# Mixing attention tokens with the images turned through DRAM, squares summed on ScalarE, and weighted products shared between VectorE and GpSimd

## The chip, the cores and the metric

The kernel runs on one core of one Trainium2 chip. The metric is the time of one execution on the device, in microseconds. The profile is one execution on that core, taken by the hardware profiler. Engines are named as the profile names them: PE is TensorE (PEld its weight loads), DVE VectorE, ACT ScalarE, POOL GpSimd, SP the queue from which nearly all DMAs are issued.

## What is computed

The reference is two layers of a "metaformer" on x of shape (4, 32, 128, 128), that is 4 batches of 32 token images of 128 x 128, all in float32. The part that matters here is the attention of the first layer. Cut down, it is

```python
tokens = x.reshape(b * t, 1, H, W)                 # x: normalised along the last axis before
tokens_norm = instance_norm(tokens, norm1_g, norm1_b)
k = fno_layer(tokens_norm, key_w, ...)             # spectral convolution + 1x1 skip, 16 heads
q = fno_layer(tokens_norm, query_w, ...)
v = fno_layer(tokens_norm, value_w, ...)
dprod = softmax(einsum('bhtd,bhsd->bhts', qf, kf) / scale)
attn = einsum('bhts,bhsd->bhtd', dprod, vf)        # tokens of a batch mixed with each other
attn = fno_layer(attn, proj_w, ...)
attn = instance_norm(attn + tokens, attn_norm_g, attn_norm_b)
m = instance_norm(attn, norm2_g, norm2_b)          # then two mixer layers, a recurrent layer,
...                                                # and the second layer of the network
```

The skip paths of value and projection make one linear map between the 32 token images of a batch: every pixel of the new image of token t is a weighted sum over the same pixel of the images s. Together with the residual this is one 128 x 128 matrix, block diagonal with a 32 x 32 block for each batch. The spectral paths add a few low Fourier coefficients to each image; they are kept as coefficients and never as images. The norms that follow need the sum of squares of each mixed image.

## The kernel before

**Layout.** XA is one SBUF tile `[128, 4, 32, 128]`: image row h on the partitions, then batch, token and column w. It holds x, then the normalised x, then the mixed images, all in place. WXY is a second large tile that holds coefficients and weights of this part: Drep (product of value and projection weights, in four head groups g, real and imaginary), Frep (the images' low coefficients, one block for each batch b), PTs (the softmax's weights), and CTbd, the block-diagonal matrix.

**Up to 134 us.** The images are loaded on SP, and in eight half batches of 16 images (`stats`, `normalise`, `transform`, lines 808 to 873) row statistics are taken, each image is normalised in place by ScalarE (L833) or VectorE (L835), and transformed by TensorE (L850). Weights are prepared beside that; their copies md, dd and m1d go by DRAM on SP. `scores` of each batch, the Gram matrix (L936), the softmax (L1004 to L1013) and PTs follow, and last CT is copied into CTbd (L1035).

**Sums stage, 134 to 205 us.** Two jobs run side by side (lines 1275 to 1304). In eight steps (g, x_) VectorE makes four products df, one for each batch, of Drep with Frep (L1290, 128 x 1088 elements, both inputs in SBUF), and TensorE sums them over heads with PTs into four accumulators ps_y (L1303, four column groups at a time). Between the products of a step, two or three times, the generator `mix` is advanced by one chunk of four image columns w:

- TensorE turns four slices `XA[:, :, :, w]` to have images on the partitions (L1050, four transposes), ScalarE copies them out as uT (L1052);
- TensorE multiplies each of the four with CTbd, the slice stationary (L1055), which turns the result back;
- ScalarE copies the 512 columns of pm into XA at stride (L1057), squares pm (L1062), and VectorE adds the square to a running sum (L1063).

`mixed_coefficients` (L1076, L1078), before step (2, 0), applies CTbd to the coefficients. Twenty chunks belong to this stage. The order on each engine is that of the program where `keep_in_program_order` says so, else the scheduler's.

**Norms stage, 205 to 244 us.** `norms` (lines 1082 to 1266) runs the list NORMS, one name after the other; inside `in_order` each compute engine keeps the order of the list (SP is not held by it). T, U, M, C, S, E with a number are a chunk's transposes, copy uT, products, copy back, square and addition for the last 12 chunks; three copies back go to VectorE (BY_VECTOR), and three chunks' squares are summed by TensorE (BY_TENSOR, L1210). The other names are the norm's own work: TY (transpose of YT, L1164), FU (L1121), VA, P0, P1, VB, D0, D1 (products and sums of coefficients on VectorE), NY (L1167) and K on GpSimd, GS and VS (sums on ScalarE, L1132 and L1155), TG (L1146), CH (the variance of every image, L1226 to L1229), PW (a power on GpSimd, L1232), E1, BC, H0, N0. EQ sums the squares over partitions with TensorE.

**After 244 us.** The list MIXERS drives the two mixer layers in eight chunks of four tokens. The first readers of mixed images are Z (L1415, which reads `XA[:, b, tokens, :]`), then TA (L1576) and R (L1583, which also reads xin, the original x, loaded again on SP from L1349). The recurrent layers and the second layer follow.

PSUM and SBUF come from pools; a pool's tile waits until what lay at its place is no longer used.

Of the kernel before, what the change touches and what calls it, by code (L numbers as in the profile page):

```python
# [32 lines left out]
P = 128  # L33
# [92 lines left out]
NORMS = """  # L126
    T31 T20 U31 M31 T27 U20 S31 C31 T24 M20 TY U24 M24 E31 U27 T23 FU C20 VA P0 S24 T28 U23 M27 S20 T26 E20 NY C24
    E24 U28 M23 M28 C23 T25 S23 U26 T29 S27 M26 E23 C27 E27 P1 U25 M25 U29 C26 T21 T30 S26 VB C28 D0 M29 K S28 E28
    U21 M21 C25 S25 U30 E26 S29 T22 D1 E25 C21 M30 WT S21 U22 GS G0 E29 M22 E21 HM W0 EQ VC TG S22 S30 VS W1 C29 E30
    C30 C22 E22 CH PW WV E1 BC H0 KG GI N0 KN  # L130
"""

BY_TENSOR, BY_VECTOR = (22, 27, 30), (21, 23, 28)
# [143 lines left out]
def _network(  # L277
# [268 lines left out]
    PTs = WXY[:, 11072:12096].rearrange("p (a b c) -> p a b c", b=4, c=P)  # L546
    gram = aw.tile([P, NT], F32, name="gram")
# [15 lines left out]
    def big(name):  # L563
        return psb.tile([P, 512], F32, tag="big", name=name)
# [233 lines left out]
    with (  # L798
# [38 lines left out]
        def transform(k):  # L837
# [34 lines left out]
            nc.scalar.copy(dst, p)  # L872
            yield True
# [92 lines left out]

        p = big("ps_s4")[:, :NB]
# [73 lines left out]
    squares = late.tile([P, 4, P], F32, name="squares")  # L1041
    mp = mixing.enter_context(tc.tile_pool(name="mix", bufs=2))
    psm = mixing.enter_context(tc.tile_pool(name="psm", bufs=2, space=PSUM))

    def mix():

        for k, w0 in enumerate(range(0, 80, 4)):
            pt = psm.tile([P, 4, P], F32, tag="pt", name="pt")
            for i in range(4):
                nc.tensor.transpose(pt[:, i, :], XA[:, :, :, w0 + i].rearrange("p b t -> p (b t)"), ident)  # L1050
            uT = mp.tile([P, 4, P], F32, name="uT")
            nc.scalar.copy(uT, pt)  # L1052
            pm = psm.tile([P, 4, P], F32, name="pm")
            for i in range(4):
                mm(pm[:, i, :], uT[:, i, :], CTbd, start=True, stop=True)  # L1055
            dst = XA[:, :, :, w0 : w0 + 4].rearrange("p b t w -> p w (b t)")
            nc.scalar.copy(dst, pm)  # L1057
            if k == 0:
                nc.scalar.square(squares, pm)
            else:  # L1060
                sq = mp.tile([P, 4, P], F32, name="sq")
                nc.scalar.square(sq, pm)  # L1062
                tt(squares, squares, sq, ALU.add)  # L1063
            yield True

    mixed = mix()
# [3 lines left out]
    def mixed_coefficients():  # L1070
        for q in halves(8, 3):
            n = q.stop - q.start
            p = psm.tile([P, 512], F32, tag="pt", name="ps_cf")[:, : 8 * n * KW].rearrange("p (a w) -> p a w", w=KW)
            for b in range(NB):
                c = slice(32 * b, 32 * b + 32)
                mm(p[c], CTbd[c, c], Frep[c, b, q].rearrange("p k r j w -> p (k r j) w"), start=True, stop=True)  # L1076
            for r in range(2):
                nc.scalar.copy(FmT.rearrange("p (r j k) w -> p r k j w", r=2, k=8)[:, r, q],  # L1078
                               p.rearrange("p (k r j) w -> p r k j w", r=2, j=4)[:, r])
        nc.vector.memset(FmT[:, 16, 0:1], 0.0)  # L1080

    def norms(np_, psn):
# [99 lines left out]
        def T(k):  # L1182
            pts[k] = psm.tile([P, 4, P], F32, tag="pt", name="pt")
            for i in range(4):
                nc.tensor.transpose(pts[k][:, i, :], XA[:, :, :, 4 * k + i].rearrange("p b t -> p (b t)"), ident)

        def U(k):
            uTs[k] = mp.tile([P, 4, P], F32, name="uT")
            nc.scalar.copy(uTs[k], pts.pop(k))

        def M(k):
            pms[k] = (psn if k % 3 == 2 else psm).tile([P, 4, P], F32, tag="pm", name="pm")
            u = uTs.pop(k)
            for i in range(4):
                mm(pms[k][:, i, :], u[:, i, :], CTbd, start=True, stop=True)

        def C(k):
            dst = XA[:, :, :, 4 * k : 4 * k + 4].rearrange("p b t w -> p w (b t)")
            if k in BY_VECTOR:
                nc.vector.tensor_copy(dst, pms[k])  # L1200
            else:
                nc.scalar.copy(dst, pms[k])

        def S(k):
            sqs[k] = mp.tile([P, 4, P], F32, name="sq")
            nc.scalar.square(sqs[k], pms[k])

        def sums(q):
            for w in range(4):
                mm(e2[:, 0:1], q[:, w], mean_mat[:, 0:1], start=(summed[0] == 0), stop=(summed[0] == summed[1] - 1))  # L1210
                summed[0] += 1

        def E(k):
            if k in BY_TENSOR:
                sums(sqs.pop(k))
            else:
                tt(squares, squares, sqs.pop(k), ALU.add)

        def EQ():
            sums(squares)  # L1220

        def CH():
            stt(var, e2[:, 0:1], 1.0 / P, var, ALU.mult, ALU.add)  # L1226
# [22 lines left out]
        def N0():  # L1249
# [4 lines left out]
                "WV": WV, "GI": GI, "T": T, "U": U, "M": M, "C": C, "S": S, "E": E, "EQ": EQ, "CH": CH, "PW": PW,  # L1254
# [22 lines left out]
    with (  # L1277
        tc.tile_pool(name="df", bufs=6) as dfp,
# [3 lines left out]
        for g in range(4):  # L1282
            for x_ in range(2):

                df = []
                if (g, x_) == (2, 0):
                    mixed_coefficients()
                for b in range(NB):
                    t = dfp.tile([P, 2, KH * KW], F32, name="df")
                    tt(t.rearrange("p r (k m) -> p r k m", k=8),  # L1290
                       Drep[:, g, :, x_].rearrange("p k j w -> p k (j w)").unsqueeze(1).broadcast_to([P, 2, 8, 4 * KW]),
                       Frep[:, b].rearrange("p k r j w -> p r k (j w)"), ALU.mult)
                    df.append(t.rearrange("p r (k m) -> p r k m", k=8))

                    if b < 2 + (x_ == 0):
                        next(mixed)
                for k in range(4):
                    r, half = divmod(k, 2)
                    m = slice(2 * KW * half, 2 * KW * (half + 1))

                    for b in range(NB):
                        c = slice(32 * b, 32 * b + 32)
                        i = mm(ys[k][c], PTs[:, 1 if (x_ == 1 and r == 0) else 0, g, c],  # L1303
                               df[b][:, r ^ x_, :, m], start=(g == 0 and x_ == 0), stop=(g == 3 and x_ == 1))
                        if k + b > 0:
                            tc.keep_in_program_order(i)
# [1107 lines left out]
```

## Time and profile before

| | us |
|---|---|
| median of 3 runs | 907.72 (907.22 to 908.0) |
| the profiled execution | 908.87 |
| its span in the profile | 907.1 |

| stretch of the span, us | PE | DVE | ACT | POOL | PE clock | GB/s |
|---|---|---|---|---|---|---|
| 100 to 120 | 19.4 | 7.7 | 7.7 | 0.0 | 1.00, 0.83 | 2 |
| 120 to 140 | 13.2 | 14.4 | 8.2 | 0.9 | 0.99, 0.50 | 1 |
| 140 to 200 | 59.2 | 45.0 | 38.4 | 0.0 | 1.00 | 1 |
| 200 to 220 | 16.1 | 16.3 | 12.3 | 7.8 | 1.00, 0.75 | 1 |
| 220 to 240 | 15.1 | 13.2 | 13.7 | 1.2 | 0.73, 0.61 | 1 |

The first table has the times; the profiled execution's own time is 1.77 us over its span, which lies around the recorded instructions. The second has busy microseconds of each engine in each stretch, the TensorE clock that was granted in its halves (1.00 is full), and what the DMA engines moved. A TensorE that shows busy is not at its peak: its instructions overlap, and four products in a row take less than four times the duration of one.

In groups of instructions below, a line gives the source line, engine, operation, output<-inputs, shapes and count; then busy us and mean ns of one; then the engine's idle time before them and what ended it. A line of a timeline gives start, duration, engine, source line, operation, and in brackets the idle time before it and its releaser. The table of stages as printed has the stretch, its length, busy us and count for PE, PEld, DVE, ACT and POOL, the granted clock, the DMA engines' busy share and GB/s.

### The profile page before, as it was taken

The numbers are of one execution on the slowest core, as the hardware profiler recorded it, in microseconds if no ns is written. First come the engines' busy times: TensorE is split into PE (matmuls) and PEld (weight loads), VectorE is DVE, ScalarE is ACT, GpSimd is POOL, SyncE is SP. The second block draws the span as 40 slices with busy tenths as digits, with TensorE's granted clock in tenths as the row PEclk, the third lists the DMA queues.
The fourth block names the chain that finished last, engine by engine and source line by source line (L and its number), as shares of the span: only waits on it lengthen the run. The fifth ranks groups of instructions, "written<-read, shape, count | busy, mean of one in ns | idle before, by whom it ended". The sixth has DMA issues, their size and how long they took to land.

```text
span 907.1 us, 31233 instructions
## 1 busy us (share of the span) xinstructions
PE 807.2 (89%) x12678; PEld 608.8 (67%) x12678; DVE 734.7 (81%) x2352; ACT 666.8 (74%) x1644; POOL 365.2 (40%) x605
## 2 busy tenths in 40 slices
PE   2999969998796989999787988999999999998994
PEld 2656557567663555564435987887878887775994
DVE  5997477777757889989988988987778887777996
ACT  2774636576682779998877997787777877776994
POOL 2000000003143454435521003788896886972263
PEclk9999979997768999999999997999999999999997
DMA  9906000000101101112100000111101111117554
GB/s 228 242 4 125 1 1 1 1 1 1 48 1 48 45 27 48 41 33 70 46 2 1 1 1 4 38 28 39 51 5 50 37 41 39 28 48 248 190 185 143
DMA packets 69419, 49.67 MB, mean 55 GB/s; under 512 B 4561, under 2 KB 64465, under 8 KB 69201
## 3 DMA queue, kind: packets, MB, share of 16 engines
q1 hardware_dynamic: 68929, 47.31, 18.5%
q8 instruction: 102, 1.67, 0.8%
q0 software_dynamic: 288, 0.01, 0.2%
q14 instruction: 52, 0.43, 0.2%
q10 hardware_dynamic: 48, 0.26, 0.1%
HBM read 30.68 MB, written 16.88 MB: 52 GB/s over the span
## 4 chain that ended last, share of the span: by engine, by line
PE 42%; DVE 23%; ACT 11%; POOL 7%; issue 4%; SPq 0%; DVEq 0%; ACTq 0%; POOLq 0%
PE ps_scan L1912 5%; PE ps_k L2065 5%; PE ps_d L2195 4%; DVE XA L1584 4%; DVE XA L1583 4%; ACT WXY L1914 3%; PE ps_y L1303 3%; PE ps_r L2065 2%; PE pm L1055 2%; POOL XN L2044 2%; PE ps_inv L481 2%; PE ps_e L2202 2%; PE ps_st L1426 2%; PE ps_w L2141 2%; ACT yw L1914 2%
## 5 line engine op out<-in xcount | busy, mean ns | idle before, releaser
L2185 DVE SCALAR_TENSOR_TENSOR U<-raw 128x512 f32<-128x512 f32 x128 | 89.6, 728 | 27.9 <-ACT raw L2177 27.6
L1913 DVE SCALAR_TENSOR_TENSOR ps_scan<-WXY,bs,ps_scan 128x128 f32<-128x128 f32 x376 | 105.7, 351 | 1.9 <-PE ps_scan L1912 1.1
L2065 PE MATMUL ps_k<-WXY,q 64*64 64x134 f32 x2048 | 86.4, 282 | 0.9 <-ACT WXY L2149 0.3
L2177 ACT COPY raw<-ps_k 128x512 f32<-128x512 f32 x128 | 71.1, 599 | 17.7 <-PE ps_k L2065 15.0
L2195 PEld LDWEIGHTS ps_d<-WXY,U 128*64 128x64 f32 x2048 | 67.3, 137 | 19.3 <-issue 12.9
L2044 POOL TENSOR_SCALAR xn<-XA,f_r,f_o 128x128 f32<-128x128 f32 x120 | 68.3, 578 | 18.7 <-PE ps_x L2065 14.0
L2044 POOL TENSOR_SCALAR XN<-XA,c_r,c_o 128x128 f32<-128x128 f32 x120 | 73.6, 622 | 5.0 <-issue 2.3
L2195 PE MATMUL ps_d<-WXY,U 128*64 128x67 f32 x2048 | 74.1, 224 | 1.0 <-ACT q L2208 0.5
L2065 PEld LDWEIGHTS ps_k<-WXY,q 64*64 64x64 f32 x2048 | 61.0, 135 | 6.7 <-DVE U L2185 0.8
L2065 PE MATMUL ps_r<-WXY,XN 64*64 64x134 f32 x1024 | 58.4, 289 | 2.4 <-DVE XN L2044 1.3
L850 PE MATMUL ps_st<-cst,XA 128*128 128x130 f32 x256 | 43.7, 311 | 14.3 <-ACT XA L833 11.2
L1641 ACT ACTIVATE xn<-XA,f_o,f_r 128x128 f32<-128x128 f32 x120 | 50.9, 489 | 4.7 <-DVE f_o L1623 4.7
L850 PEld LDWEIGHTS ps_st<-cst,XA 128*128 128x128 f32 x256 | 35.4, 207 | 27.4 <-ACT XA L833 12.3
L1420 ACT ACTIVATE Z<-Z,k,aB 128x128 f32<-128x128 f32 x128 | 51.1, 481 | 3.5 <-DVE Z L1415 3.2
L1583 DVE SCALAR_TENSOR_TENSOR XA<-ps_inv,r1B,xin 128x128 f32<-128x128 f32 x128 | 44.1, 345 | 8.9 <-PE ps_inv L1576 8.9
L1584 DVE SCALAR_TENSOR_TENSOR XA<-Z,gB,XA 128x128 f32<-128x128 f32 x128 | 46.5, 364 | 5.0
L2163 ACT COPY q<-ps_r 128x512 f32<-128x512 f32 x64 | 38.4, 599 | 12.6 <-PE ps_r L2065 12.3
L2024 POOL TENSOR_TENSOR c_r<-c_e,neg_half 128x16 f32<-128x16 f32 (+2 forms) x10 | 25.6, 2564 | 53.6 <-DVE c_e L2017 53.5
L496 PE MATMUL ps_inv<-invq,cst 64*128 64x512 f32 x128 | 41.9, 685 | 4.6 <-ACT invq L487 3.9
L1290 DVE TENSOR_TENSOR df<-WXY 128x1088 f32<-128x1088 f32 x32 | 40.2, 1288 | 2.1 <-PE ps_y L1303 2.1
L2202 PE MATMUL ps_e<-WXY,q 128*64 128x67 f32 x1024 | 41.1, 222 | 0.0
L446 PE MATMUL ps_wx<-xt,wvt 128*128 128x512 f32 x64 | 35.6, 639 | 5.8 <-ACT WXY L453 4.5
(459 smaller groups left out, 2253.7 us busy)
## 6 DMA issues: line engine op xcount, KB each, us to landing
XA<-in_x_dram SPq DMA_DIRECT2D x16, 512.0 KB, 7.1
xin<-in_x_dram SPq DMA_DIRECT2D x32, 256.0 KB, 3.4
turned<-XA SPq DMA_DIRECT2D x32, 256.0 KB, 2.3
out_dram<-res SPq DMA_DIRECT2D x52, 128.0 KB, 2.1
XA<-turned SPq DMA_DIRECT2D x6, 1024.0 KB, 12.2
WXY<-dd SPq DMA_DIRECT2D x4, 544.0 KB, 11.2
XA<-turned SPq DMA_DIRECT2D x6, 256.0 KB, 12.3
out_dram<-resl SPq DMA_DIRECT2D x12, 128.0 KB, 2.1
```

The costliest lines, as they stand in the source:

```text
L850: mm(p[:, i, :], XA[:, b, t0 + j + i, :], cst[:, C_E : C_E + 130], start=True, stop=True)
L1420: nc.scalar.activation(z, z, AF.Gelu, bias=k1, scale=aB[:, j : j + 1])
L1583: stt(a, p2[c, b][:, i], r1B[:, j : j + 1], xin[c, b - b % 2][:, b % 2, i], ALU.mult, ALU.add)
L1584: stt(a, Z[c][:, b, i], gB[c][:, n : n + 1], a, ALU.mult, ALU.add)
L1641: nc.scalar.activation(t[:, dst, :], a, AF.Identity, bias=sh, scale=sc_)
L1913: stt(p4, WX[:, :, h, :], s[:, 0:1], p4, ALU.mult, ALU.add)
L2044: e.tensor_scalar(dst, src_, r, o, ALU.mult, ALU.add)
L2065: m = mm(dst, data, taps, start=(n == 0 and (i, j) not in last), stop=(n == 1), skip_group_check=True)
L2177: nc.scalar.copy(raw[u, k], banks["k", u][:, k])
L2185: stt(U[u][:, k].rearrange("p k s m -> p (k s m)"), v, SLOPE, v, ALU.mult, ALU.max)
L2195: mm(p[HALVES[s], m, b, REACH[k]], U[v][:, b, k, s, HALVES[m]], DR[:, k, REACH[k]], start=(m == 0 and b == 0 and k == 0), stop=(k == 1), s ...
L2202: mm(p[HALVES[j], b * P : b * P + P][:, REACH[m]], q3[v - 1][:, m, b, HALVES[j]], DC[:, m, REACH[m]], start=(b == 0 and m == 0), stop=(m = ...
```

## The change

It rewrites how the images are mixed and who makes the products df. In the text the steps are named by the letters of the new lists.

- **Turning.** Each half batch, once normalised, is also stored to a DRAM tile `normed` (n, h, w). After the last, eight loads of 1 MB bring it back into XA with the images on the partitions: the view XR is `[128 images, 128 rows h, 128 w]`. A chunk k is now four image rows: M is one product, CTbd stationary and 512 columns of XR moving. C copies it back in place; after every 16 rows a 1 MB store takes them to a second DRAM tile, `mixed`. XB, 32 loads of 256 KB, brings all images back with rows h on the partitions, after the last store.
- **Squares.** S squares pm on ScalarE with `accum_out`, one column of `squares` for each chunk; images are on the partitions, so EQ is one reduce of 32 numbers on VectorE.
- **Products.** F n.b is product df of step n and batch b. All of step 0 and batch 3 of every step go to GpSimd, 11 of 32, the others to VectorE. Eight buffers instead of six. Y n.k is one accumulator's part of the sums of step n.
- **Order.** A list SUMS sets the order of the sums stage on every compute engine, and NORMS is written anew. CF is `mixed_coefficients`. XB stands behind S31.

```diff
+SUMS = """
+    F0.3 F0.0 F0.1 F0.2 M0 M1 M2 F1.3 F1.0 F1.1 F1.2 Y0.0 Y0.1 C0 S0 M3 Y0.2 Y0.3 C1 S1 M4 F2.3 F2.0 F2.1 F2.2 Y1.0
+    C2 S2 M5 Y1.1 Y1.2 C3 S3 M6 Y1.3 C4 S4 M7 F3.3 F3.0 F3.1 F3.2 Y2.0 Y2.1 C5 S5 M8 Y2.2 Y2.3 C6 S6 M9 F4.3 F4.0
+    F4.1 F4.2 Y3.0 C7 S7 M10 Y3.1 Y3.2 C8 S8 M11 Y3.3 C9 S9 M12 F5.3 F5.0 F5.1 F5.2 Y4.0 Y4.1 C10 S10 M13 Y4.2 Y4.3
+    C11 S11 M14 CF F6.3 F6.0 F6.1 F6.2 Y5.0 C12 S12 M15 Y5.1 Y5.2 C13 S13 M16 Y5.3 C14 S14 M17 F7.3 F7.0 F7.1 F7.2
+    Y6.0 Y6.1 C15 S15 M18 Y6.2 Y6.3 C16 S16 M19 Y7.0 C17 S17 M20 Y7.1 Y7.2 C18 S18 M21 Y7.3 C19 S19
+"""
 NORMS = """
...
+    TY C20 S20 M22 FU C21 S21 M23 VA C22 S22 M24 P0 NY C23 S23 M25 P1 C24 S24 M26 VB C25 S25 M27 D0 C26 S26 M28 K D1
+    C27 S27 M29 WT C28 S28 M30 GS C29 S29 M31 G0 C30 S30 HM W0 C31 S31 XB EQ VC TG VS W1 CH PW WV E1 BC H0 KG GI N0
+    KN
 """
-BY_TENSOR, BY_VECTOR = (22, 27, 30), (21, 23, 28)
+ROWS = 16
...
+    normed, mixed = (scratch.tile([P, P, P], F32, name=k) for k in ("normed", "mixed"))
+    XR = XA.rearrange("p b t w -> p (b t) w")
...
+            n0 = b * NT + t0
+            nc.sync.dma_start(normed[n0 : n0 + HB].rearrange("n h w -> h n w"), XA[:, b, t0 : t0 + HB, :])
             yield True
...
+        for h in range(0, P, ROWS):
+            nc.sync.dma_start(XR[:, h : h + ROWS, :], normed[:, h : h + ROWS, :])
...
-    def mix():
...
+    psm = mixing.enter_context(tc.tile_pool(name="psm", bufs=4, space=PSUM))
+    squares = late.tile([P, NT], F32, name="squares")
+    junk = late.tile([P, 512], F32, name="junk")
+    pms = {}
+
+    def mix(k):
+        pms[k] = psm.tile([P, 512], F32, tag="pm", name="pm")
+        mm(pms[k], CTbd, XR[:, 4 * k : 4 * k + 4, :].rearrange("p h w -> p (h w)"), start=True, stop=True)
+
+    def mix_copy(k):
+        nc.scalar.copy(XR[:, 4 * k : 4 * k + 4, :].rearrange("p h w -> p (h w)"), pms[k])
+        if (4 * k + 4) % ROWS == 0:
+            h = slice(4 * k + 4 - ROWS, 4 * k + 4)
+            nc.sync.dma_start(mixed[:, h, :], XR[:, h, :])
+
+    def mix_square(k):
+        nc.scalar.activation(junk, pms.pop(k), AF.Square, accum_out=squares[:, k : k + 1])
...
+    def images_back():
+        for t in range(0, NT, TM):
+            for b in range(NB):
+                n = b * NT + t
+                nc.sync.dma_start(XA[:, b, t : t + TM, :], mixed[n : n + TM].rearrange("n h w -> h n w"))
...
-        def T(k):
...
         def EQ():
-            sums(squares)
+            nc.vector.tensor_reduce(total, squares, AX.X, ALU.add)

         def CH():
-            stt(var, e2[:, 0:1], 1.0 / P, var, ALU.mult, ALU.add)
+            stt(var, total, 1.0 / P**2, var, ALU.mult, ALU.add)
...
-        tc.tile_pool(name="df", bufs=6) as dfp,
+        tc.tile_pool(name="df", bufs=8) as dfp,
...
+        def weighted(n, b):
+            g, x_ = steps[n]
+            t = dfp.tile([P, 2, KH * KW], F32, name="df")
+            (nc.gpsimd if n == 0 or b == NB - 1 else nc.vector).tensor_tensor(
+                t.rearrange("p r (k m) -> p r k m", k=8),
+                Drep[:, g, :, x_].rearrange("p k j w -> p k (j w)").unsqueeze(1).broadcast_to([P, 2, 8, 4 * KW]),
+                Frep[:, b].rearrange("p k r j w -> p r k (j w)"), ALU.mult)
+            df[n, b] = t.rearrange("p r (k m) -> p r k m", k=8)
+
+        def summed(n, k):
+            g, x_ = steps[n]
+            r, half = divmod(k, 2)
+            m = slice(2 * KW * half, 2 * KW * (half + 1))
+            for b in range(NB):
+                c = slice(32 * b, 32 * b + 32)
+                mm(ys[k][c], PTs[:, 1 if (x_ == 1 and r == 0) else 0, g, c],
+                   df[n, b][:, r ^ x_, :, m], start=(n == 0), stop=(n == len(steps) - 1))
+
+        with in_order():
+            for piece in SUMS.split():
...
```

More of the change, by code (lines that the diff above doesn't have):

```diff
@@ L119 @@
 """
+SUMS = """
[5 more added lines that the diff above has]
+"""
 NORMS = """
[L127 to L130, printed above, removed]
+    TY C20 S20 M22 FU C21 S21 M23 VA C22 S22 M24 P0 NY C23 S23 M25 P1 C24 S24 M26 VB C25 S25 M27 D0 C26 S26 M28 K D1
+    C27 S27 M29 WT C28 S28 M30 GS C29 S29 M31 G0 C30 S30 HM W0 C31 S31 XB EQ VC TG VS W1 CH PW WV E1 BC H0 KG GI N0
+    KN
 """
-BY_TENSOR, BY_VECTOR = (22, 27, 30), (21, 23, 28)
+ROWS = 16
 MIXERS = """
@@ L546, in _network @@
     PTs = WXY[:, 11072:12096].rearrange("p (a b c) -> p a b c", b=4, c=P)
+    scratch = att.enter_context(tc.tile_pool(name="scratch", bufs=1, space=bass.MemoryType.DRAM))
+    normed, mixed = (scratch.tile([P, P, P], F32, name=k) for k in ("normed", "mixed"))
+    XR = XA.rearrange("p b t w -> p (b t) w")
     gram = aw.tile([P, NT], F32, name="gram")
@@ L1040, in _network @@
     late = mixing.enter_context(tc.tile_pool(name="late", bufs=1))
-    squares = late.tile([P, 4, P], F32, name="squares")
-    mp = mixing.enter_context(tc.tile_pool(name="mix", bufs=2))
-    psm = mixing.enter_context(tc.tile_pool(name="psm", bufs=2, space=PSUM))
-    def mix():
[L1047 to L1066, printed above, removed]
+    psm = mixing.enter_context(tc.tile_pool(name="psm", bufs=4, space=PSUM))
[12 more added lines that the diff above has]
+        nc.scalar.activation(junk, pms.pop(k), AF.Square, accum_out=squares[:, k : k + 1])
     FmT = late.tile([P, 2 * KH, KW], F32, name="FmT")
@@ L1072, in mixed_coefficients @@
             n = q.stop - q.start
-            p = psm.tile([P, 512], F32, tag="pt", name="ps_cf")[:, : 8 * n * KW].rearrange("p (a w) -> p a w", w=KW)
+            p = psm.tile([P, 512], F32, tag="pm", name="ps_cf")[:, : 8 * n * KW].rearrange("p (a w) -> p a w", w=KW)
             for b in range(NB):
@@ L1095, in norms @@
         pool, pools = nc.gpsimd.tensor_tensor, nc.gpsimd.tensor_scalar
-        pts, uTs, pms, sqs = {}, {}, {}, {}
         e2 = psn.tile([P, 512], F32, name="ps_e2")
-        summed = [0, 4 + 4 * len(BY_TENSOR)]
+        total = np_.tile([P, 1], F32, name="total")
         def weighted(o, total, t):
@@ L1179, in GI @@
             ts(gI, ident, scalar("attn_norm_g"), None, ALU.mult)
-        def T(k):
[L1183 to L1217, printed above, removed]
         def EQ():
-            sums(squares)
+            nc.vector.tensor_reduce(total, squares, AX.X, ALU.add)
         def CH():
-            stt(var, e2[:, 0:1], 1.0 / P, var, ALU.mult, ALU.add)
+            stt(var, total, 1.0 / P**2, var, ALU.mult, ALU.add)
             ts(vs[:, 1:2], var, g2e, 1e-10, ALU.mult, ALU.add)
@@ L1253, in norms @@
                 "HM": HM, "TG": TG, "VA": VA, "VB": VB, "VS": VS, "VC": VC, "W1": W1, "TY": TY, "NY": NY, "WT": WT,
-                "WV": WV, "GI": GI, "T": T, "U": U, "M": M, "C": C, "S": S, "E": E, "EQ": EQ, "CH": CH, "PW": PW,
+                "WV": WV, "GI": GI, "M": mix, "C": mix_copy, "S": mix_square, "EQ": EQ, "XB": images_back, "CH": CH, "PW": PW,
                 "E1": E1, "BC": BC, "H0": H0, "N0": N0}
@@ L1281, in _network @@
         ys = [psy.tile([P, 8, 2 * KW], F32, name=f"ps_y{k}") for k in range(4)]
[L1282 to L1286, printed above, removed]
-                    mixed_coefficients()
[L1288 to L1306, printed above, removed]
@@ new lines, in _network @@
+        df, steps = {}, [(g, x_) for g in range(4) for x_ in range(2)]
+        def weighted(n, b):
[6 more added lines that the diff above has]
+            df[n, b] = t.rearrange("p r (k m) -> p r k m", k=8)
@@ new lines, in summed @@
+        def summed(n, k):
[8 more added lines that the diff above has]
+            for piece in SUMS.split():
+                if piece == "CF":
+                    mixed_coefficients()
+                    continue
+                name = piece.rstrip("0123456789.")
+                {"F": weighted, "Y": summed, "M": mix, "C": mix_copy, "S": mix_square}[name](
+                    *map(int, piece[len(name) :].split(".")))
```

## The prediction

> **What bounds the kernel now.** I read the table of stages first (busy time per engine over stretches of the span), then for the two stages that the diff touches the chain of work, the groups of instructions and the timeline. The touched part runs from 133.2 us, when the weights of attention are final, to 244.4 us, when the first mixer reads a mixed image. Everything later (663 us) is untouched. The chain over the start of that part, and the costliest groups from 133.5 to 205 us:
>
> ```profile
> by line: PE pm L1055 41.0%; PE ps_y L1303 27.8%; PE pt L1050 22.1%; ACT sq L1062 2.6%; DVE WXY L1018 2.3%; ACT XA L1057 2.3%; ACT uT L1052 1.7%; issue 1.4%
> ```
>
> ```profile
> L1290 DVE TENSOR_TENSOR df<-WXY 128x1088 f32<-128x1088 f32 x32 | 40.2, 1288 | 2.1 <-PE ps_y L1303 2.1
> L1303 PE MATMUL ps_y<-df,WXY 128*32 128x272 f32 x256 | 27.8, 397 | 0.0
> L1057 ACT COPY XA<-pm 128x512 f32<-128x512 f32 x20 | 21.2, 1059 | 17.7 <-PE pm L1055 17.7
> L1063 DVE TENSOR_TENSOR squares<-squares,sq 128x512 f32<-128x512 f32 x19 | 13.1, 690 | 13.0 <-ACT sq L1062 12.9
> L1062 ACT ACTIVATE sq<-pm 128x512 f32<-128x512 f32 x19 | 12.3, 645 | 0.0
> ```
>
> Three engines share this stage: VectorE has 53 us of work in 70 (df and squares), ScalarE about 51, and TensorE runs transposes, products and sums in one queue; each waits for another in turn (ACT 17.7 us for pm, DVE 12.9 us for sq). No engine is full, and the ring of waits costs 8.9 us a step (eight steps in 71 us). The second stage, 205.2 to 244.4 us, ends like this:
>
> ```profile
> 205.21 2.31 DVE L1164 STREAM_TRANSPOSE WXY<-YT 128x2048 f32<-128x2048 f32 x1 [0.53 <-ACT YT L1314]
> ...
> 231.78 2.31 DVE L1146 STREAM_TRANSPOSE WXY<-HT 128x2048 f32<-128x2048 f32 x1
> ...
> 232.25 2.81 ACT L1202 COPY XA<-pm 128x512 f32<-128x512 f32 x3
> ...
> 244.37 0.75 DVE L1415 SCALAR_TENSOR_TENSOR Z<-XA,sc,ps_inv 128x512 f32<-128x512 f32 x1 [0.77 <-PE ps_inv L496]
> ```
>
> From the end of the second transpose (234.1) to Z a chain of small steps takes 10.3 us; the change leaves it alone. What comes before is the remaining 11 to 12 chunks of the mixing, threaded through VectorE's norm work: the last three copies back stand at 232.25 beside the second transpose, so both lists end together there.
>
> The change puts the same kind of product on GpSimd and on VectorE at once, so I looked for a place where both now read SBUF together:
>
> ```profile
> 207.62 3.13 POOL L1167 TENSOR_SCALAR WXY<-WXY 128x1024 f32<-128x1024 f32 x1 [2.00 <-DVE WXY L1164]
> 208.02 2.15 DVE L1121 TENSOR_TENSOR FuT<-FmT,YT 128x1088 f32<-128x1088 f32 x1
> ...
> 210.40 1.29 DVE L1149 TENSOR_TENSOR V<-FmT,FuT 128x1088 f32<-128x1088 f32 x1
> ```
>
> The same VectorE shape takes 2.15 us beside a GpSimd instruction and 1.29 alone: 0.86 lost to the neighbour.
>
> **What the Trainium skill says.** "SBUF — State Buffer", section "Who interferes with whom": a VectorE instruction with two SBUF inputs contends with a GpSimd instruction that reads SBUF, and the pair of ports is an exclusive lock, not a division of bandwidth. The lines above agree (2.15 against 1.29); so does the line L2044 on GpSimd, 0.44 us at the median and up to 1.73. "GPSIMD Engine Reference", section 3.1: a two-input elementwise instruction of 2048 takes 4497 ns there, about 2.2 ns an element. The trace agrees: GpSimd products of 128 take 454 ns (L1509 to L1511), of 256 726 ns (L2264), 2.1 ns an element; for 1088 that extends to 0.73 + 832 x 0.00212 = 2.5 us. "TensorE: Matmul & The Clock Gate", "What's actually happening": an idle TensorE runs at half clock until busy again; in the trace the granted clock is 0.50 from 130 to 140 us, after the softmax's gap, 1.00 from 140 to 210, and 0.61 to 0.75 from 210 to 240, where gaps return.
>
> **The change part by part.**
>
> *Turning by DRAM.* 128 transposes (four take 0.58 us) and 32 copies uT (0.59 us) go; four products (0.55 us) become one of 512 columns (two at L1576 take 1.06, so 0.53). ScalarE's copy back is contiguous: 0.60 us, as raw<-ps_k (L2177), for 1.06; its store waits on SP, where only later stores stand behind it. The square stays at 0.64 and gains an accumulator read of 0.20 (as at L1132). ScalarE falls from 2.29 to 1.44 us a chunk, about 1.2 of it in time, since neighbours overlap (eight of 481 ns, L1420, take 2.85). VectorE loses all 28 additions (0.69 each) and three copies (1.02), TensorE the 32 products that summed squares (L1210, 5.5 us); a reduce of 32 numbers, EQ, is new.
>
> *First turn.* Eight stores of 1 MB go on SP between 30 and 100 us, ahead there of the dd copies, which are needed only at 135; eight 1 MB loads follow the last store. The loads at the start, in rows of 512 bytes as well, moved 277 GB/s:
>
> ```profile
> 20.00:40.00 20.00, 18.39 (x116) 12.99 (x118) 17.80 (x89) 13.93 (x34) 0.00 (x0) 1.00 1.17 277
> ```
>
> (the last column of the table of stages). So the last store, issued near 100, lands by 106, and the loads take 8.39 MB / 277 GB/s = 30 us more: first chunk near 111, last near 140. The first product comes at 135, the last quarter after 190. Cost nothing, under the cover of scores and softmax; without that cover a product would wait for its chunk, with Y queued behind it on TensorE, and the turn would show with some 25 us. What waits on SP behind the stores (dd, m1d, the zeros of hankel) is late by at most one half batch, and its readers come after 135, the taps of hankel (95.9) apart, whose zeros stand behind the fifth store (near 75).
>
> *Sums stage.* 21 of 32 df products stay on VectorE (1.29), 11 go to GpSimd (2.5; the bounds are 2.3, the slope with no fixed cost, and 3.0, by the 2.76 ns an element of L1396 with its short rows). I take the lock as full, so both share one clock: 21 x 1.29 + 11 x 2.5 = 54.6 us against 53.3 before. All four of step 0 are on GpSimd; in the compiled program its first product waits for the copies of CT (135.1), since its buffers lie where the softmax's did, so they don't hide behind the softmax. VectorE's three of step 1 share the port with them: 135.1 + 10.0 + 3.9 = 149.0. Y0 and M3 take 3.1 us at full clock and 4.1 at three quarters, which I take, since TensorE now has gaps: 153.1. Buffers (8, two steps) free there, and steps 2 to 7 cost 3 x 1.29 + 2.5 = 6.4 each, 38.2 us: 191.3. CF, three groups of products with ScalarE copies between them, stands ahead of Y5 and holds the buffers that step 7 needs: 3 us. Y7 with its two M: 4.6. So Y ends at 199, the YT copies at 199.6, where 205.2 stood: 5.6 us gained. ScalarE (20 x 1.2 = 24) and TensorE (about 5 us a step) lie beside it.
>
> *Norms stage*, from the YT transpose. ScalarE: 12 x 1.2 = 14.4, GS 1.25, and 0.5 waiting for VectorE's D1 (its list: 2.3, 2.2, 0.2, 1.2, 1.3, 1.3, 1.2, 0.65, 0.65, with K's small steps 11.3): the last square ends at +16.2. Then EQ 0.25, VC 0.2, transpose 2.3: +18.95; with the unchanged 10.3, Z at +29.2, for 39.2 before. 10.0 us gained.
>
> *Second turn.* The last copy back ends at +15.4 (215.0). Its 1 MB store takes 3.8 us and some 2 of landing (the 256 KB stores to turned land in 2.3 us): 221. The first 256 KB return lands in 3.4 (as xin does): 224, before Z at 228.8. The other 31 take 30 us; xin, now behind them on SP, lands near 258, and the first residual that reads it, at 276.4 before, comes at 260.8. Cost nothing, with 3 us of margin.
>
> Sum: 5.6 + 10.0 = 15.6 us. The profiled execution took 908.87 (span 907.1); the median of the runs is 907.72, 1.15 less. 908.87 - 15.6 = 893.3, less 1.15: 892.
>
> **The rivals.**
> A, the case above, 892, own range 885 to 899 (df on GpSimd at 2.3 to 3.0, 11 of them, gives -2 to +5.5; the clock -2 to +2).
> B, the lock does not hold between these products, VectorE and GpSimd overlap. Step 0 is ready at 145, then each step costs 4 to 5 us (TensorE 2.5 + 2.5 x 0.53 at full to three-quarter clock): Y ends near 187 instead of 199, 880. For it: the lock is seen on single pairs only. Against it: the 0.86.
> C, the return is late: at 210 GB/s (the last tenth of the kernel shows 143 to 248 on mixed traffic) 8.39 MB and 1 MB of xin take 45 us, and the residuals wait 7 to 8 us: 900. Against it: the 277 measured with the same 512-byte rows.
> D, slower: GpSimd's product. It decides from 2.5 + 15.6 / 11 = 3.9 us. If its 16 short rows and the repeated operand double it to 5.0, the shared port carries 27 us more: 919. For it: L1396, slow with short rows. Against it: L1509, rows of 32 with a repeated operand at 454 ns.
>
> **How the numbers follow.** A 0.63, B 0.14, C 0.12, D 0.11 (0.03 of it near no change). Within 0.2% (1.8 us) is what measuring this kernel can't tell from no change: faster 0.89, same 0.03, slower 0.08. The range of 8 in 10 takes A and C and half of B: 878 to 903.
>
> **What would show it.** VectorE's 128x1088 products at sums of 1.3 and more than 2 us beside GpSimd's, few at 1.29 throughout (B); the YT transpose near 200 and Z near 229; GpSimd's product alone near 2.5; no wait of the residual for xin; TensorE idle before Y, released by df. Wrong would make it: a wait of M for a DMA, the first Z waiting for XA, or GpSimd's products running while VectorE's take 1.29.

## The result, and the profile after

The changed kernel takes 898.42 us at the median of eight runs (894.23 to 904.07); the kernel before, run beside it, 907.80. The ratio is 0.990 with a 95% interval of 0.987 to 0.993: faster by 9.4 us (1%), where 15.6 were forecast. The profiled execution took 895.1 us (span 893.3), where the sum of the prediction gave 893.3. So most of the miss lies between the profiled execution and the median, and only 1.8 us in the sum itself; but that the sum came out so near is luck, since an error of +5.5 met errors of -2.6, -0.8 and -0.3.

The span is cut at three events that exist in every kernel here: CT final (the last of the four small copies that end the softmax), the start of the transpose of YT (all sums done), and the first Z (the first mixer reads a mixed image).

| us | CT final at | CT to YT transpose | to the first Z | Z to the end | span |
|---|---|---|---|---|---|
| before | 135.2 | 70.0 | 39.2 | 662.7 | 907.1 |
| forecast | 135.1 | 64.5 | 29.2 | 662.7 | 891.5 |
| after | 140.6 | 61.9 | 28.4 | 662.4 | 893.3 |

The stage of the sums became 8.1 us shorter and the norms 10.8; the part ahead of them, which the prediction had left alone, became 5.4 us longer. First the products df, from the page of the changed kernel:

```profile
L1261 DVE TENSOR_TENSOR df<-WXY 128x1088 f32<-128x1088 f32 x21 | 44.0, 2159 | 12.5 <-PE ps_y L1274 12.5
L1261 POOL TENSOR_TENSOR df<-WXY 128x1088 f32<-128x1088 f32 x11 | 35.7, 3255 | 27.6 <-PE ps_y L1274 17.7
```

The same VectorE product had a mean of 1288 ns before; now 2159. The means hide two populations. The same line in three stretches of 5 us from CT on, minimum, median and maximum of each engine's instructions:

```profile
L1261 DVE TENSOR_TENSOR df<-WXY x2: 1292/2436/3581, 140.6 to 141.8; 128x1088 f32<-128x1088 f32 x2
L1261 POOL TENSOR_TENSOR df<-WXY x2: 3454/3490/3527, 140.8 to 144.2; 128x1088 f32<-128x1088 f32 x2
```

```profile
L1261 DVE TENSOR_TENSOR df<-WXY x2: 3570/3576/3581, 141.8 to 145.3; 128x1088 f32<-128x1088 f32 x2
L1261 POOL TENSOR_TENSOR df<-WXY x2: 3523/3525/3527, 144.2 to 147.7; 128x1088 f32<-128x1088 f32 x2
```

```profile
L1261 POOL TENSOR_TENSOR df<-WXY x3: 2478/2484/3523, 147.7 to 153.7; 128x1088 f32<-128x1088 f32 x3
```

Alone a product takes 1.28 us on VectorE and 2.48 on GpSimd. Side by side both records show 3.5 to 3.6 us: each contains the other's whole work (1.28 + 2.48 = 3.76, less a little overlap at the edges). Had they shared the port at half speed, the VectorE product would have ended after some 2.6 us (an estimate, twice 1.28). The engines take turns, and the busy column of either counts the other's turn as its own.

The chain of work over the stage then names who ends last there:

```profile
by line: PE pm L1064 27.2%; PE ps_y L1274 25.0%; POOL df L1261 20.8%; DVE df L1261 13.6%; issue 4.2%; PE ps_cf L1083 4.0%; ACT FmT L1085 2.6%; ACT junk L1073 1.0%; ACT XA L1067 0.9%; ACT YT L1292 0.5%; DVE WXY L1050 0.3%; POOLq L1261 0.1%; 
```

A third of the stage is the port (df on both engines), and GpSimd's part of it alone is 20.8%: these 12.88 us are the first step's four products, before which TensorE has no sum to do. More than half is TensorE.

Now the part ahead of CT. The waits from 84 to 120 us of the changed kernel have two lines that the kernel before does not have:

```profile
DVE fsq L757 <- DMA F<-in_dn_dram: 3.0, 1, 3.0
PE ps_f L767 <- DVE frows L763: 2.8, 1, 2.8
```

and the DMA list for 84 to 104 us shows what it waited for (last column: median us from issue to landing; this line read 2.0 before):

```profile
normed<-XA SPq DMA_DIRECT2D x2, 1024.0 KB, 6.6
F<-in_dn_dram POOLq DMA_DIRECT2D x2, 0.3 KB, 6.0
```

F holds the taps of one resampling filter, 0.3 KB, and has nothing to do with the attention. It is issued at 88.4 on GpSimd's queue. What the DMA engines carry just then, from 88 to 91 us, first in the changed kernel, then before:

```profile
DMA packets 158, 0.62 MB, mean 206 GB/s; under 512 B 16, under 2 KB 16, under 8 KB 158
DMA packets 64, 0.00 MB, mean 1 GB/s; under 512 B 64, under 2 KB 64, under 8 KB 64
```

The stores to normed have packets of 512 bytes, and none of those is there: 142 of the 158 have 2 to 8 KB and belong to the copies of dd and m1d (544 KB in 128 rows, 4352 bytes each). A store of 1 MB stood ahead of these copies on SP (from 75 to 76 us 489 packets under 2 KB; before, 49 of 2 to 8 KB), so they began near 79 us for 75, and nearly all of them were done by 91.9 for 87.4. F's own packets start at 93.0, 1.1 us after that; before, where F was issued as the copies ended (87.6), they start 1.2 us after the issue. So the stores delay F by way of the copies that they push back. This is read from the packets; no run moves the copies alone. VectorE, in order, stands 3.0 us at the first instruction that reads F; TensorE runs dry behind it. Stretches of 2 us (columns: engines' busy time, then clock, DMA share, GB/s):

```profile
94.00:96.00 2.00, 0.26 (x5) 0.25 (x5) 1.08 (x7) 0.68 (x3) 0.00 (x0) 1.00 1.04 299
96.00:98.00 2.00, 2.00 (x10) 1.47 (x10) 2.00 (x15) 0.48 (x1) 0.00 (x0) 0.57 1.03 286
98.00:100.00 2.00, 2.00 (x11) 1.60 (x8) 1.26 (x8) 1.44 (x4) 0.00 (x0) 0.50 1.02 286
100.00:102.00 2.00, 2.00 (x11) 1.71 (x10) 2.00 (x5) 1.09 (x4) 0.56 (x1) 0.50 1.04 293
```

TensorE does 0.26 us of work in 94 to 96, and then its clock is 0.50 from 96.3 to 103.1, while it is busy nearly throughout. Before, this stretch ran at 1.00 throughout. Three microseconds of waiting became five and a half at CT.

The norms, in the chain of work:

```profile
202.54 2.32 DVE WXY L1177
...
204.95 3.71 POOL WXY L1180
...
212.77 0.57 POOL cc L1125
213.37 1.22 ACT V L1145 x2
214.59 0.47 ACT XA L1067
...
217.19 0.60 ACT junk L1073 x2
217.82 0.19 DVE total L1196
218.00 0.12 DVE g L1171
218.12 2.22 DVE WXY L1159
```

Last square, sum, second transpose: at +15.3, +15.5 and +17.8 us from the YT transpose, for 16.2, 16.5 and 19.0 forecast. And the second turn is not on the path: the first residual (L1561, which reads xin) starts at 261.75, 30.9 us after Z (32.0 before), and what it waits for is its product on TensorE.

### The profile page after: what moved, and what is told of

Same layout as the page of the kernel before. It is cut to its first block, busy times and chain, and to the rows that moved or that the text cites. A ratio compares the mean times of both kernels' runs of the same rounds, so it can differ in the third digit from the quotient of the medians.

```text
span 893.3 us, 30568 instructions
## 1 busy us (share of the span) xinstructions
PE 771.3 (86%) x12326; PEld 557.4 (62%) x12326; DVE 718.7 (80%) x2311; ACT 642.3 (72%) x1647; POOL 402.9 (45%) x616
## 4 chain that ended last, share of the span: by engine, by line
PE 36%; DVE 24%; ACT 13%; POOL 9%; issue 4%; SPq 0%; DVEq 0%; ACTq 0%; POOLq 0%
PE ps_k L2043 5%; PE ps_d L2173 4%; DVE XA L1562 4%; PE ps_scan L1890 4%; DVE XA L1561 4%; ACT WXY L1892 4%; ACT yw L1892 3%; PE ps_r L2043 2%; PE ps_st L1404 2%; POOL XN L2022 2%; PE ps_e L2180 2%; PE pm L1064 2%; PE ps_inv L488 2%; PE ps_w L2119 2%; PE ps_y L1274 2%
## 5 line engine op out<-in xcount | busy, mean ns | idle before, releaser
L2163 DVE SCALAR_TENSOR_TENSOR U<-raw 128x512 f32<-128x512 f32 x128 | 89.6, 728 | 27.8 <-ACT raw L2155 27.6
L2155 ACT COPY raw<-ps_k 128x512 f32<-128x512 f32 x128 | 71.2, 599 | 17.9 <-PE ps_k L2043 15.5
L2022 POOL TENSOR_SCALAR XN<-XA,c_r,c_o 128x128 f32<-128x128 f32 x120 | 75.5, 640 | 4.8 <-issue 2.2
L860 PE MATMUL ps_st<-cst,XA 128*128 128x130 f32 x256 | 46.0, 323 | 15.5 <-ACT XA L843 12.4
L860 PEld LDWEIGHTS ps_st<-cst,XA 128*128 128x128 f32 x256 | 37.5, 218 | 29.0 <-ACT XA L843 13.6
L1261 DVE TENSOR_TENSOR df<-WXY 128x1088 f32<-128x1088 f32 x21 | 44.0, 2159 | 12.5 <-PE ps_y L1274 12.5
L1561 DVE SCALAR_TENSOR_TENSOR XA<-ps_inv,r1B,xin 128x128 f32<-128x128 f32 x128 | 44.1, 344 | 9.2 <-PE ps_inv L1554 9.2
L1261 POOL TENSOR_TENSOR df<-WXY 128x1088 f32<-128x1088 f32 x11 | 35.7, 3255 | 27.6 <-PE ps_y L1274 17.7
L503 PE MATMUL ps_inv<-invq,cst 64*128 64x512 f32 x128 | 41.1, 669 | 4.5 <-ACT invq L494 3.7
## 6 DMA issues: line engine op xcount, KB each, us to landing
XA<-normed SPq DMA_DIRECT2D x8, 1024.0 KB, 16.2
```

Of the source, the lines that this page charges most:

```text
L860: mm(p[:, i, :], XA[:, b, t0 + j + i, :], cst[:, C_E : C_E + 130], start=True, stop=True)
L1261: (nc.gpsimd if n == 0 or b == NB - 1 else nc.vector).tensor_tensor(t.rearrange("p r (k m) -> p r k m", k=8), Drep[:, g, :, x_].rearrange( ...
L1561: stt(a, p2[c, b][:, i], r1B[:, j : j + 1], xin[c, b - b % 2][:, b % 2, i], ALU.mult, ALU.add)
L2022: e.tensor_scalar(dst, src_, r, o, ALU.mult, ALU.add)
L2155: nc.scalar.copy(raw[u, k], banks["k", u][:, k])
L2163: stt(U[u][:, k].rearrange("p k s m -> p (k s m)"), v, SLOPE, v, ALU.mult, ALU.max)
```

## The experiments

Eleven runs, the changed kernel once more and ten edits of it, each timed beside the kernel before. First the stages of all of them, from one profiled execution each, and the medians of 4 to 14 executions:

| us | CT final at | CT to YT transpose | to Z | Z to end | median (range) |
|---|---|---|---|---|---|
| after | 140.6 | 61.9 | 28.4 | 662.4 | 898.4 (894.2 to 904.1) |
| again | 138.9 | 62.7 | 28.8 | 661.9 | 898.5 (894.2 to 902.5) |
| dn_early | 135.4 | 62.3 | 28.5 | 665.6 | 891.9 (890.7 to 893.6) |
| no_turn1 | 135.7 | 62.4 | 28.5 | 661.6 | 892.2 (889.6 to 894.1) |
| all_dve | 139.6 | 47.9 | 28.4 | 665.5 | 879.8 (876.6 to 883.2) |
| pool8 | 142.5 | 58.5 | 27.6 | 663.6 | 897.1 (894.1 to 899.5) |
| no_turn2 | 139.1 | 63.4 | 29.1 | 668.8 | 900.9 (897.2 to 902.5) |
| pe_turn | 135.9 | 70.2 | 34.4 | 661.5 | 902.7 (902.2 to 903.8) |
| sq_dve | 139.8 | 68.6 | 33.0 | 661.2 | 905.3 (904.5 to 912.5) |
| dve_dn | 134.5 | 47.9 | 28.5 | 665.9 | 878.6 (874.9 to 879.5) |
| dve_dn_pre | 135.9 | 47.5 | 27.8 | 663.7 | 876.5 (873.9 to 877.8) |
| best24 | 135.9 | 50.6 | 25.0 | 663.4 | 877.0 (875.7 to 880.8) |

Where an edit did not touch them, the sums (61.9 to 63.4) and the norms (27.6 to 29.1) agree within 1.5 us; "Z to end" does not (661 to 669), of which more below. CT falls into two groups: 138.9 to 142.5 in the six kernels in which F is late, 134.5 to 135.9 in the others and before. So the stages decide, and the medians are read with some 3 us of doubt.

**again: the changed kernel once more.**

> The changed kernel once more, for its scatter: its runs lay between 894 and 904 us with a mean clock of 0.935 to 0.946, where those of before lay within 1.6 us. If the scatter belongs to the kernel, the runs spread over 8 us or more again and the long ones have the lower clock, median 896 to 901. If it belonged to the chip of the first job, they lie within 2 us.

Median 898.49, runs from 894.23 to 902.52 with clocks of 0.942 to 0.933. The spread belongs to the kernel. Its profiled execution (894.23) was the fastest of its runs.

**dn_early: the small load out of the way of the stores.**

```
-            F = wp.tile([n, 2, 12], F32, tag="F", name="F")
-            for j in range(2): ... nc.gpsimd.dma_start(F[:, j, :], ...)      # inside the loop over k
+        Fs = [wp.tile([n, 2, 12], F32, tag=f"F{k}", name="F") for k in range(2)]
+        for k in range(2): ... nc.gpsimd.dma_start(Fs[k][:, j, :], ...)      # ahead of it
```

> The 0.3 KB of dn are loaded at the start, into a buffer of their own, and no longer between the stores of the images. If the late landing of this small load (VectorE 3.0 us idle at 92 to 95 us, TensorE after it at half clock for 7 us) is what made the softmax end 5.5 us later than before, CT is final at 135 to 136.5 us for 140.6, and the median falls by 4 to 5 us. Rival: the stores and loads slow other work of the early stage (ports, queues), and the wait only shows it: CT stays at 139 or later and the time falls by less than 2 us.

CT is final at 135.4, and the median falls by 6.6 us to 891.9. From 88 to 114 us the clock is 1.00, though the stores are the same (279 GB/s). The rival falls: the traffic as such delays neither CT nor the median. The range shrinks to 2.9 us.

**no_turn1: the first turn left out.**

```
-            nc.sync.dma_start(normed[n0 : n0 + HB].rearrange("n h w -> h n w"), XA[:, b, t0 : t0 + HB, :])
...
-        for h in range(0, P, ROWS):
-            nc.sync.dma_start(XR[:, h : h + ROWS, :], normed[:, h : h + ROWS, :])
```

> The first turn is left out: nothing is stored to normed or loaded from it, and the products M read the images as they lie, so the mixed values are wrong. If the only cost of the first turn is the late small load, CT is final near 135 to 136 us and the time falls by 4 to 5 us, as with dn loaded early. If the traffic costs more than that, through slower instructions or the clock, the fall is larger, 6 to 10 us, and the scatter of the runs goes with it.

CT at 135.7, median 892.2, as with dn loaded early: 17 MB of traffic less buys no more than moving a load of 0.3 KB. F lands in 1.9 us here. Beyond that wait and its clock, no cost of the first turn shows.

**all_dve: nothing on GpSimd.**

```
-            (nc.gpsimd if n == 0 or b == NB - 1 else nc.vector).tensor_tensor(
+            nc.vector.tensor_tensor(
```

> All 32 products df on VectorE, nothing on GpSimd; the order of all else is kept. If products of the two engines exclude each other at the SBUF port, the stage needs 32 x 1.28 = 41 us of the port for 21 x 1.28 + 11 x 2.48 = 54 us, TensorE's 40 us stand beside it, and the YT transpose starts 46 to 50 us after CT is final for 61.9: the time falls by 11 to 15 us. Rival: GpSimd takes real work from VectorE and the stage is bound by TensorE and ScalarE or by the order written out; then it starts 60 us or more after CT and the time is the same or up to 8 us longer.

The stage takes 47.9 us for 61.9. The 32 products, over the stage:

```profile
L1261 DVE TENSOR_TENSOR df<-WXY 128x1088 f32<-128x1088 f32 x32 | 38.7, 1285 | 2.2 <-PE ps_y L1274 2.2
```

All take 1.285 us on average (32 x 1.285 = 41.1; the column counts overlapping edges once), and VectorE waits 2.2 us in all for a free buffer. So giving 11 products to a second engine had cost 14 us. The chain over the stage no longer has df in it:

```profile
by line: PE pm L1064 51.2%; PE ps_y L1274 37.4%; issue 5.9%; PE ps_cf L1083 5.2%; DVE WXY L1177 4.8%; ACT FmT L1085 3.4%; POOL HT L1100 1.9%
```

TensorE now ends last, with 94% of it. The median falls by 18.7, more than the 11 to 15 expected, though the stage gives 14 to 15 and the profiled spans differ by 10.9 (892.3 and 881.4; this profile is the slowest of its five executions). Where the medians' other 4 us come from is not shown.

**pool8: a third of the way.**

```
-            (nc.gpsimd if n == 0 or b == NB - 1 else nc.vector).tensor_tensor(
+            (nc.gpsimd if b == NB - 1 else nc.vector).tensor_tensor(
```

> Only the fourth product of each step stays on GpSimd (8 of 32); the first step's other three go back to VectorE. If the port is exclusive, the products take 24 x 1.28 + 8 x 2.48 = 50.6 us of it for 54.2, and the first step is ready 6 us after CT for 13: the YT transpose starts 55 to 59 us after CT for 62, the time falls by 3 to 7 us, about a third of what all 32 on VectorE give. Rival: GpSimd's share is a relief; then it is the same or longer.

The stage takes 58.5 us: 3.4 to 4.2 less. The median falls by 1.3 us only, short of the 3 to 7 expected and within the scatter of both kernels; in the profiled execution CT came later (142.5 for 138.9 and 140.6), and the stage is what the edit touches. The time of the port, n x 1.28 + m x 2.48, is 54.2 us with 11 products on GpSimd and 50.6 with 8, and the stage is 7.7 and 7.9 longer. (With none it is 41.1, and the stage 6.8 longer; but there TensorE ends last, so that is no third test.)

**sq_dve: the squares summed by VectorE again.**

```
-        nc.scalar.activation(junk, pms.pop(k), AF.Square, accum_out=squares[:, k : k + 1])
...
+        nc.scalar.square(sq, pms.pop(k))
+        tt(squares, squares, sq, ALU.add)
```

> The sum of squares goes back to VectorE: ScalarE squares a chunk, VectorE adds it (0.69 us) and waits for it in its own order; turn and df as in the changed kernel. If VectorE's port is what bounds the stage of the sums, 20 additions lengthen it by 14 us or more, with the waits for ScalarE up to 20, and the norms by 0 to 4: the time rises by 14 to 22 us. Rival: the additions fall into VectorE's 12 us of waiting: it rises by less than 5.

Between the two expectations: +6.7 us in the sums, +4.6 in the norms, +6.8 at the median. The groups of the stage show how:

```profile
L1078 DVE TENSOR_TENSOR squares<-squares,sq 128x512 f32<-128x512 f32 x19 | 19.8, 1040 | 1.0
L1077 ACT ACTIVATE sq<-pm 128x512 f32<-128x512 f32 x20 | 12.3, 613 | 22.2 <-DVE squares L1078 22.2
```

The additions (0.69 us alone, 1.04 here beside GpSimd) add 19 x 0.69 = 13.1 us to the port: 67.3, and the stage is 68.6. By this sum the port is nearly full; in the changed kernel it stood free for 7.7 us (61.9 less 54.2), and half of the additions went there.

**pe_turn: the turn alone undone.** Transposes on TensorE, uT, four products a chunk, the strided copy back, no traffic with DRAM. (With them come one buffer fewer for pm and CF one place earlier.)

```
-        mm(pms[k], CTbd, XR[:, 4 * k : 4 * k + 4, :].rearrange("p h w -> p (h w)"), start=True, stop=True)
...
+            nc.tensor.transpose(pt[:, i, :], XA[:, :, :, 4 * k + i].rearrange("p b t -> p (b t)"), ident)
+        nc.scalar.copy(uTs[k], pt)
...
+            mm(pms[k][:, i, :], u[:, i, :], CTbd, start=True, stop=True)
```

> The turn by way of DRAM alone is undone: four transposes on TensorE, the copy uT, four products of 128 columns and the strided copy back, as before; squares by ScalarE and the split of df stay. If the turn brings what the sum said, ScalarE takes 1.05 us more a chunk: 3 to 8 us in the stage of the sums, 10 to 12 in the norms, and the softmax ends 5 us earlier for want of the stores: 905 to 912 us. Rival: the gain of the change lies in the squares, and the turn, with what its stores cost, brings nothing: 893 to 899.

+8.3 us in the sums, +6.0 in the norms, CT 4.7 earlier. The chain over the stage of the sums, and ScalarE in it:

```profile
by line: PE pm L1077 22.5%; PE ps_y L1284 22.0%; PE pt L1065 20.6%; POOL df L1271 18.4%; ACT XA L1080 5.5%; PE ps_cf L1093 3.6%; ACT junk L1083 2.9%; ACT uT L1067 2.3%; ACT FmT L1095 1.5%; ACT YT L1302 0.8%; issue 0.6%; POOLq L1271 0.1%
```

```profile
L1080 ACT COPY XA<-pm 128x512 f32<-128x512 f32 x21 | 22.8, 1087 | 0.0
L1083 ACT ACTIVATE junk<-pm 128x512 f32<-128x512 f32 x21 | 13.8, 659 | 0.0
L1067 ACT COPY uT<-pt 128x512 f32<-128x512 f32 x23 | 13.6, 590 | 21.6 <-PE pt L1065 21.6
```

ScalarE has 1.087 + 0.590 us a chunk for the 0.600 of the changed kernel's copy, but in this stage it waits 21.6 us for TensorE's transposes: TensorE is 69% of the chain, and the transposes alone are 20.6%. In the norms ScalarE's list does end last (its copies and squares are 60% of that chain). The median, 902.7, lies between the two expectations: the norms gave back 6 of the 10 to 12, in part because ScalarE stands waiting for 3.1 us there in the changed kernel, and here its longer list fills that wait. Against dn_early, the turn without the late F, the turn by DRAM is worth 10.8 us at the medians.

**no_turn2: the second turn left out.**

```
-            nc.sync.dma_start(mixed[:, h, :], XR[:, h, :])
...
-    C27 S27 M29 WT C28 S28 M30 GS C29 S29 M31 G0 C30 S30 HM W0 C31 S31 XB EQ VC TG VS W1 CH PW WV E1 BC H0 KG GI N0
+    C27 S27 M29 WT C28 S28 M30 GS C29 S29 M31 G0 C30 S30 HM W0 C31 S31 EQ VC TG VS W1 CH PW WV E1 BC H0 KG GI N0
```

> The second turn is left out: mixed is neither stored nor loaded back, so the mixer reads images that lie turned, and its values are wrong. If the return is hidden, the YT transpose to Z stays at 28.4 us, the residual follows Z after 31 us as before, and the time is the same within 2 us. Rival: the return holds Z or xin up, or slows VectorE's and ScalarE's work: it falls by 3 us or more.

No stage up to Z became shorter, and the residual still follows Z after 31.6 us. The return is hidden. The median is 2.4 us higher, slightly outside the 2 us expected, through the part after Z (668.8), in which nothing was edited but the transfers ahead of it.

**dve_dn: both cures.** The edits of all_dve and dn_early together.

> Both cures at once: all 32 products on VectorE and dn loaded at the start. If the two costs are separate, the stages are those of the two single edits: CT final at 135.4, 48 us to the YT transpose, 28.4 to Z, 662 to 666 after it: 874 to 879 us. If they hide one another (a later start of the stage was partly covered), it stays at 879 or more.

878.55, stages as in the single edits: in the stages the two costs are separate. At the medians it gains only 1.3 over all_dve, where the profiled executions differ by 4.7 (883.24 and 878.55); the ranges overlap, so the medians do not confirm it.

**dve_dn_pre and best24: what bounds the stage now.** Three products of the first step go into VectorE's idle time ahead of the softmax, with nine buffers of which three stand by themselves; best24 adds four more chunks of the mixing to the stage.

```
+        for b in range(NB - 1):
+            weighted(0, b)
         p = big("ps_s4")[:, :NB]
...
-    F0.3 F0.0 F0.1 F0.2 M0 M1 M2 F1.3 ...
+    F0.3 M0 M1 M2 F1.3 ...
```

> As dve_dn, and three of the first step's four products, into buffers that no earlier tile uses, stand in VectorE's idle time at 106 to 114 us, ahead of the softmax. If VectorE's products still bound the stage, it is 3 x 1.28 = 3.8 us shorter, 44 us: 870 to 875. Rival: TensorE (sums and products, about 41 us) bounds it by now, and it gains less than 1.5 us.

> As dve_dn_pre, with 24 of the 32 chunks of the mixing in the stage of the sums for 20. If ScalarE's list still bounds the norms, its 12 chunks of 1.2 us become 8: the norms take 25 to 26 us for 28.4, the sums 0 to 2 more for four products on TensorE: 867 to 873 us. Rival: the chain of the norms on VectorE and GpSimd takes over and nothing is gained.

In dve_dn_pre the rival holds: 47.5 us for 47.9, though 3.8 us of products are gone. In best24 the norms shrink by 2.8 us, to the 25 that were expected, but the sums grow by 3.1 where 0 to 2 were expected, and nothing is gained. The chain over the stage of dve_dn_pre:

```profile
by line: PE pm L1079 53.3%; PE ps_y L1279 35.7%; PE ps_cf L1098 5.3%; DVE WXY L1192 4.9%; ACT FmT L1100 3.4%; POOL HT L1115 1.9%; issue 0.5%
```

94% of it is TensorE; VectorE's products are off the path. So four more chunks there cost TensorE's time for their products (up to 4.2 us, at 1.06 each). dve_dn_pre, at 876.45 (ratio to before 0.965, interval 0.963 to 0.967), beats both kernels by far; the three best are within 2.1 us of each other and can't be told apart.

## Why the prediction was right in its course and wrong in three terms

*What bounded the stage before.* Misread. "No engine is full" stands beneath a chain that is 91% TensorE. Busy time of PE, PEld, DVE, ACT and POOL before, from CT to the YT transpose, then clock, DMA share and GB/s:

```profile
135.20:205.20 70.00, 69.18 (x541) 46.21 (x539) 52.09 (x55) 45.16 (x72) 0.48 (x1) 0.97 0.00 1
```

TensorE was busy for 69 of 70 us and ended last; VectorE, which the change relieved, was not what the stage waited for. What shortens the stage is above all TensorE's work that goes: undoing the turn puts 8.3 us back, with the transposes on the chain.

*The lock and the sums.* Right in mechanism and size. Port: 54.6 us forecast, 54.2 measured (2.5 and 2.48 for GpSimd's product). First step ready 13.1 us after CT for 13.9; third step's products start at +18.4 for +18.0; YT transpose at +61.9 for +64.5, since the six steps from there, with CF among them, took 38.1 us where 41.2 were forecast (six of 6.4, and 3 for CF). The Trainium skill's "SBUF — State Buffer", "Who interferes with whom", says that the shared pair of ports is an exclusive lock, and that a VectorE instruction with two SBUF inputs contends there with a GpSimd instruction that reads SBUF; the records agree (1.28 becomes 3.57). Rivals B and D are out: no overlap, and GpSimd's product is 2.48, far from 3.9. What the prediction did not ask is what the same lock says of the part itself: if the two share one clock, the slower engine has to lose. That was in its own numbers (32 x 1.29 = 41 against 54.6). The forecast came near although the stage before was misread, because with 11 products on GpSimd the port sets the pace of the steps, as pool8 and all_dve show.

*TensorE's product.* Mis-sized. "Two at L1576 take 1.06, so 0.53" takes for two products what are the two instructions of one float32 product; M takes 1.06 us ("197.84 1.06 PE pm L1064 x2" in the chain). The four products that it replaced are 8 instructions a chunk (160 for 20), about 1.1 us, so the step "four products become one" brings nothing, as it said, at twice the size. In this kernel it was hidden behind the port; in dve_dn_pre, where TensorE ends the stage 47.5 us after CT, it is on the path.

*Norms.* 28.4 for 29.2: the last square came at +15.3 for +16.2, in part by luck. GS was forecast at +11.3 and started at +10.8, but ScalarE waited 3.1 us for it where 0.5 were forecast: it had done two of its twelve chunks before the YT transpose, and a chunk took 1.08 us in time for 1.2. The profile puts the wait down to GpSimd's small steps (cc, until 213.3); VectorE's D1, which GS reads, ended at 213.3 as well. After it came GS and the three chunks written behind it. best24 has no chunk behind GS, eight in the norms for twelve, and saves 2.8.

*First turn, "cost nothing".* Wrong, and the step that failed: "late by at most one half batch, and its readers come after 135". The copies of dd and m1d were late by just that, some 4 us, and their own readers did not mind; but transfers of other queues were not asked about, and F, on GpSimd's, came to stand behind the copies. The Trainium skill's "DMA: Bandwidth & Descriptors", "Issuing engines are not separate DMA queues", says that DMAs started by ScalarE, SyncE or GpSimd all run on the same 16 DMA engines and interleave. That they share the engines the traces show: F lands in 2.0 us where the copies have just ended (before; 1.9 in no_turn1), and in 5.6 to 6.1 where they still run. F's packets did interleave with those of the stores, but hardly with those of the copies: the first of them starts when nearly all of the copies' are done. The loads themselves were easier than forecast: 410 to 428 GB/s in stretches of 4 us where 277 was taken, done near 134 for 140.

*Second turn, "cost nothing".* Right (no_turn2), and rival C is out.

*From the profiled execution to the median.* The sum was off by 1.8 us (+5.5, -2.6, -0.8, -0.3); the other 4.5 us of the miss is that the median lies 3.3 above the profiled execution where before it lay 1.15 below. The kernel before has a spread of 1.6 us (1.8 to 3.5 in its executions beside the other runs); this one, 10. The times go roughly with the mean clock: 904.07 at 0.935, 894.23 at 0.945, though again has 894.23 at 0.938. The Trainium skill's "TensorE: Matmul & The Clock Gate", "What's actually happening", says that the gate looks at a free-running window of 3413 ns. In the traces the half-clock stretch after the late F lasts one such window (96.3 to 99.7 in again), two (96.3 to 103.1 in after) or three (96.4 to 106.6 in pool8), and CT goes with it: 138.9 and 139.1 us with one (again, no_turn2), 139.6 to 140.6 with two (all_dve, sq_dve, after), 142.5 with three (pool8). These kernels are the same up to CT, so the same late F costs 3.7 to 7.3 us against the 135.2 of before. Without it the range is 2.9 us. But it isn't all: no_turn1 spreads over 4.5, all_dve 6.7, no_turn2 5.2, and the part after Z varies from 661 to 669 us between kernels that are the same there. What tips those windows was not settled: no run here separates it, since only one execution of each kernel has a trace.

So the change is three parts of unlike sign, in stages of the profiled executions: turn by DRAM 8.3 + 6.0 us gained, less 4.7 for the late F; squares on ScalarE 6.7 + 4.6 gained; df on GpSimd 14.0 lost. (Each is measured with the other two in place, so they do not add up to the whole. The new order and the eight buffers are in all these kernels; no run takes them back alone.)

## What to carry to other kernels

Before work is given to a second engine, ask first whether the first one is what ends last: here the chain of the kernel before named TensorE. Then ask whether both read through the same port, and if so add up the port and not the engines: the slower one then makes the total longer, however idle it looks. When large transfers are put beside existing work, list what they push back and the small loads of every queue in that time, and load those ahead; the wait of 3 us for F cost 3.7 to 7.3 us at CT, with TensorE at half clock after it. And a busy column that has grown without new work is a wait in disguise: look at the minimum of the same shape.

## What was not expected of the hardware

- A product on GpSimd and one on VectorE, each with two SBUF inputs, exclude each other for whole instructions: both records show 3.5 to 3.6 us, near the sum of 2.48 and 1.28.
- A DMA of 0.3 KB took 5.6 to 6.1 us to land when copies with packets of 4352 bytes were in flight on another queue, 2.0 when they had just ended. In the changed kernel its packets started 1.1 us after nearly all of the copies' were done, and then moved beside stores at some 330 GB/s.
- The half-clock stretch after one and the same wait of 2.6 to 3.0 us lasted 3.4, 6.8 or 10.2 us in six executions.
- Reading turned rows back in pieces of 16 rows (8 KB a partition) ran at 410 to 428 GB/s (114 to 130 us, in stretches of 4 us); the stores of the same size, in rows of 512 bytes, at 286 to 335 (92 to 102 us, in stretches of 2).
